# A state space scan: drive by diagonal matmuls on TensorE for half of the groups, and the sum over states by identity matmuls

## Chip, cores, metric

One core of a Trainium2 chip (trn2). The metric is the device time of one execution in microseconds (us), the median of several.

## The reference, cut to what matters

Two layers on an input of 4 x 384 x 64 x 64, all in f32. The first is a state space (Mamba) layer over L = 4096 positions, with 768 inner channels and 16 states each; the second is a neighbourhood attention. Only the first is touched. Its core, after projections and a short convolution that give dt, B, C and xc:

```python
def step(h, inp):
    dt_t, B_t, C_t, x_t = inp
    dA  = jnp.exp(dt_t[:, :, None] * A[None])              # "decay"
    dBx = (dt_t * x_t)[:, :, None] * B_t[:, None, :]       # "drive"
    h   = dA * h + dBx                                     # the scan over positions
    y_t = jnp.einsum('bdn,bn->bd', h, C_t)                 # product with C, sum over the 16 states
    return (h, y_t)
```

## The kernel before

The layer is worked off in 64 *steps* (4 batches x 16 chunks of T = 256 positions). In each, channels lie on the 128 partitions in ND = 6 tiles d, and the 16 states in four groups g of NG = 4. A pair m = (d, g) is one group; each group is scanned in two halves of two states, so that a step has 48 *slots*, one per half. All other work of the layer (projections, convolution, normalization of the coming chunks) is written into a plan that says in which slot it is issued; engines keep that order.

For each group: ScalarE makes the decay, one exponential per state, into PSUM; VectorE or GpSimd makes the drive (dt x) * B; VectorE scans; GpSimd multiplies by C; TensorE sums over the states.

```python
def driven(I, m, h, eng):                      # 15 of 24 on VectorE, 9 on GpSimd
    d, g = divmod(m, NS // NG)
    db = w2.tile([P, NG, T], F32, tag="db", name=f"db_{I}_{m}", bufs=6)
    dtx = dtx_ps[:, d % 2, :] if eng is nc.vector else h["dtx"][d]
    eng.tensor_tensor(db, dtx.unsqueeze(1).broadcast_to([P, NG, T]), h["B"][g], ALU.mult)
    dbs[I, m] = db

def decay(I, m, half, h):
    d, g = divmod(m, NS // NG)
    da = ps_a.tile([P, 2, T], F32, tag="da", name="da")          # PSUM
    for k in range(2):
        n = g * NG + 2 * half + k
        act(da[:, k, :], h["dt"][d // 2][:, d % 2, :], AF.Exp, scale=nega[:, d, n : n + 1])
    das[I, m, half] = da

def scans(I, m, half, hs): ...                 # tensor_tensor_scan(hs, da, db, state, mult, add)
def with_c(I, m, h, hs): ...                   # GpSimd: last state kept; hs = hs * C

def summed(I, m, h, hs):                       # transposes that accumulate in PSUM
    ...
    for k in range(NG):
        for half in range(2):
            nc.tensor.matmul(
                y[:, d % 2, half, :], hs[:, k, half * P : (half + 1) * P], ident,
                is_transpose=True, start=..., stop=..., skip_group_check=True,
            )
# turn(): ScalarE copies the turned sum to SBUF, TensorE turns it back and adds D * xc
```

Transposes by an identity that accumulate in one PSUM bank add the states up, turned; one more transpose for each pair of tiles turns the result back.

## Time and profile before

| | us |
|---|---|
| time, median of all its runs beside the changed kernel's | 8368.6 (8366.0 to 8371.4) |
| layer 0, one step of 64 | 92.4 |
| start and layer 1 | some 2450 |

The busy line and three groups of the page show who does what. PE is TensorE, PEld its weight loads, DVE VectorE, ACT ScalarE and POOL GpSimd; the granted clock, met below, is the share of its full clock that TensorE was given. A group's line gives the operation, output and inputs, shapes, count, busy time and the mean length of one, then the idle time before it.

```profile
PE 7252.0 (87%) x45882; PEld 5495.0 (66%) x45882; DVE 7311.7 (87%) x13300; ACT 5812.2 (70%) x13758; POOL 7092.7 (85%) x5719
```

```profile
L571 DVE TENSOR_TENSOR_SCAN hs<-da,state,db 128x256 f32<-128x256 f32 x5760 | 3855.0, 728 | 88.9 <-ACT da L96 64.8
...
L594 PE MATMUL y<-ident,hs 128*128 128x128 f32 x12288 | 1774.6, 296 | 904.5 <-POOL hs L581 902.3
...
L550 DVE TENSOR_TENSOR db<-dtx_ps,B 128x1024 f32<-128x1024 f32 x960 | 1141.3, 1199 | 0.0
```

The two averages of 87% come from different layers. The scans take the most VectorE time, the drive (L550) comes second there, and that is what the change takes away. The sum (L594) mostly waits for GpSimd.

### The profile page before, as it was taken

To read this page: it belongs to the slowest core of one execution; us is meant where nothing else is said; L and a number is where in the kernel's file an instruction comes from. 1 tells how busy PE (TensorE), PEld (TensorE's weight loads), DVE (VectorE), ACT (ScalarE), POOL (GpSimd) and SP (SyncE) were. 2 spreads that over 40 slices of the span, in tenths; PEclk is the share of its full clock that TensorE was granted. 3 is DMA by queue.
4 is the path that set the end of the run, shared out by engine and by line. 5 is a ranking of instruction groups with operands and counts; after the bars stand their busy time and mean duration, and the time that the engine had idled before them with its cause. 6 is when DMAs were issued, how large, how long until landed. Compare 5 with 4: busy or idle time off the path is not lost. (4 is left out here: it accounts for less than half of the span.)

```text
span 8357.8 us, 139186 instructions
## 1 busy us (share of the span) xinstructions
PE 7252.0 (87%) x45882; PEld 5495.0 (66%) x45882; DVE 7311.7 (87%) x13300; ACT 5812.2 (70%) x13758; POOL 7092.7 (85%) x5719
## 2 busy tenths in 40 slices
PE   7888888888888888888888888888699999999999
PEld 5776677777666677776777677766555555555555
DVE  5999999999999999999999999999856666666666
ACT  5777777777777777777777777777545455455455
POOL 4999999999999999999999999999767677777677
PEclk9998898889889998899898889989799999999999
DMA  3111211121112111211211111112122232232222
GB/s 112 59 61 66 75 58 55 63 74 58 62 66 74 53 58 66 72 58 64 68 63 53 58 65 60 55 57 71 65 89 86 76 94 88 78 92 85 83 87 65
DMA packets 327504, 583.06 MB, mean 70 GB/s; under 512 B 62940, under 2 KB 211180, under 8 KB 326660
## 3 DMA queue, kind: packets, MB, share of 16 engines
q1 hardware_dynamic: 326788, 574.17, 21.3%
q8 instruction: 370, 6.06, 0.3%
q14 instruction: 346, 2.83, 0.1%
HBM read 471.49 MB, written 84.73 MB: 67 GB/s over the span
## 5 line engine op out<-in xcount | busy, mean ns | idle before, releaser
L571 DVE TENSOR_TENSOR_SCAN hs<-da,state,db 128x256 f32<-128x256 f32 x5760 | 3855.0, 728 | 88.9 <-ACT da L96 64.8
L96 ACT ACTIVATE da<-dt,nega 128x256 f32<-128x256 f32 x6144 | 2917.7, 477 | 1208.2 <-DVE hs L571 1100.8
L581 POOL TENSOR_TENSOR hs<-hs,C 128x1024 f32<-128x1024 f32 x1536 | 3621.7, 2358 | 123.9 <-POOL state L580 0.4
L594 PE MATMUL y<-ident,hs 128*128 128x128 f32 x12288 | 1774.6, 296 | 904.5 <-POOL hs L581 902.3
L594 PEld LDWEIGHTS y<-ident,hs 128*128 128x128 f32 x12288 | 1540.5, 153 | 1207.9 <-POOL hs L581 1098.9
L941 POOL TENSOR_SCALAR sg<-sg,rsum 128x308 f32<-128x308 f32 x1536 | 1619.9, 1073 | 633.8 <-DVE rsum L939 631.8
L550 POOL TENSOR_TENSOR db<-dtx,B 128x1024 f32<-128x1024 f32 x576 | 1360.5, 2362 | 0.1
L550 DVE TENSOR_TENSOR db<-dtx_ps,B 128x1024 f32<-128x1024 f32 x960 | 1141.3, 1199 | 0.0
L382 PE MATMUL mm_ps<-xn,w_in 128*128 128x256 f32 x4608 | 1127.4, 392 | 10.1 <-DVE yg L624 8.1
L96 ACT ACTIVATE sg<-sg,mx 128x308 f32<-128x308 f32 x1536 | 828.7, 541 | 251.3 <-DVE mx L926 236.7
L926 DVE CUSTOM_DVE_ANT_0 sg<-lg_ps,bias 128x308 f32<-128x308 f32 x1536 | 643.1, 475 | 375.1 <-PE lg_ps L920 375.1
L382 PEld LDWEIGHTS mm_ps<-xn,w_in 128*128 128x128 f32 x4608 | 872.5, 197 | 119.1 <-DVE yg L624 8.4
L389 PE MATMUL mm_ps<-xb,dcv 128*128 128x256 f32 x3072 | 783.9, 409 | 0.0
L389 PEld LDWEIGHTS mm_ps<-xb,dcv 128*128 128x128 f32 x3072 | 615.7, 208 | 88.3 <-issue 0.3
L969 ACT COPY tb<-pt_ps 88x512 f32<-88x512 f32 x384 | 222.2, 579 | 624.7 <-PE pt_ps L965 624.7
L580 POOL COPY state<-hs 128x4 f32<-128x4 f32 x1536 | 289.1, 188 | 341.8 <-DVE hs L571 328.0
L639 PE MATMUL mm_ps<-yg,w_out 128*128 128x256 f32 x2304 | 539.8, 385 | 0.0
L956 DVE COPY ta<-pt_ps 110x512 f32<-110x512 f32 x768 | 492.4, 682 | 23.2 <-PE pt_ps L951 23.2
L639 PEld LDWEIGHTS mm_ps<-yg,w_out 128*128 128x128 f32 x2304 | 439.6, 195 | 59.1
L951 PE MATMUL pt_ps<-ident,sg 128*110 128x128 f32 x3072 | 417.7, 279 | 0.8 <-POOL sg L941 0.8
L951 PEld LDWEIGHTS pt_ps<-ident,sg 128*110 128x110 f32 x3072 | 322.7, 133 | 77.9 <-issue 47.6
L824 PE MATMUL mm_ps<-xn,w_qkv 128*128 128x512 f32 (+2 forms) x612 | 270.7, 579 | 60.4 <-DVE xn L811 53.2
(141 smaller groups left out, 9152.5 us busy)
## 6 DMA issues: line engine op xcount, KB each, us to landing
B<-bcrows SPq DMA_DIRECT2D x256, 512.0 KB
C<-bcrows SPq DMA_DIRECT2D x256, 512.0 KB
vw<-vd SPq DMA_DIRECT2D x1792, 33.0 KB
xr<-x SPq DMA_DIRECT2D x28, 1056.0 KB
vd<-v SPq DMA_DIRECT2D x280, 96.0 KB
xi<-in_x_dram SPq DMA_DIRECT2D x64, 384.0 KB
xo<-in_x_dram SPq DMA_DIRECT2D x64, 384.0 KB
x<-xo SPq DMA_DIRECT2D x64, 384.0 KB
```

The costliest lines, as they stand in the source:

```text
L96: ins = nc.scalar.activation(o, i, func, **kw)
L382: nc.tensor.matmul(pb[:, k, :], w_in[:, j, m * P : (m + 1) * P], xn[:, j, :], start=(j == 0), stop=(j == NJ - 1),)
L389: nc.tensor.matmul(pb[:, k, :], dcv[:, d, c, :], xb[:, d, c : c + T], start=(c == 0), stop=(c == KC - 1),)
L550: eng.tensor_tensor(db, dtx.unsqueeze(1).broadcast_to([P, NG, T]), h["B"][g], ALU.mult)
L571: nc.vector.tensor_tensor_scan(hs[:, j, :], da[:, k, :], dbs[I, m][:, j, :], state[:, d, n : n + 1] if I % NCHUNK else 0.0, ALU.mult, ALU.add,
L581: nc.gpsimd.tensor_tensor(hs, hs, h["C"][g], ALU.mult)
L594: nc.tensor.matmul(y[:, d % 2, half, :], hs[:, k, half * P : (half + 1) * P], ident, is_transpose=True, start=(first and half == 0 and d % ...
L639: nc.tensor.matmul(h["po", first][:, m - first, :], w_out[:, d, m * P : (m + 1) * P], h["yg"][d // 2][:, d % 2, :], start=(d == 0), stop=( ...
L926: nc.vector.tensor_tensor_reduce(sg[:, hh, :], lg[:, :NK], bias[:, 4 * m + hh, :], -1.0, BIG, ALU.add, ALU.min, mx[:, hh : hh + 1],)
L941: nc.gpsimd.tensor_scalar(sg[:, hh, :], sg[:, hh, :], rs[:, hh : hh + 1], None, ALU.mult)
L951: nc.tensor.transpose(pt[: KN[c], col : col + P], sg[:, 2 * pair + hh, KOFF[c] : KOFF[c] + KN[c]], ident,)
L956: nc.vector.tensor_copy(t[: KN[0], :, :].rearrange("p a q -> p (a q)"), pt[: KN[0], :])
```

## The change

Its intent: VectorE is full in layer 0, so let TensorE make the drive of groups 0 and 2. (dt x) * B over positions t is a matmul of the turned dt x with a diagonal matrix of B, which leaves the drive in PSUM; the decay of these groups then goes to SBUF. The sum over states becomes a matmul by the identity, which needs no turning back.

```diff
-            ps_a = es.enter_context(tc.tile_pool(name="ps_a", bufs=2, space=PSUM))
-            ps_x = es.enter_context(tc.tile_pool(name="ps_x", bufs=1, space=PSUM))
+            ps_a = es.enter_context(tc.tile_pool(name="ps_a", bufs=3, space=PSUM))
...
+            ON_PE = (0, 2)
...                                   # the plan: input projections some seven slots later
-                    ((-10, -9, -6), (1, 2, 5), (9, 10, 13)),
+                    ((-3, -2, 1), (4, 5, 8), (11, 12, 15)),
...                                   # diagonal(g), twice a step, VectorE
+                    nc.vector.tensor_tensor(
+                        h["dg", g],
+                        ident.unsqueeze(1).unsqueeze(1).broadcast_to([P, 2, NG, P]),
+                        h["BT", g][:, :, r0 : r0 + NG].unsqueeze(3).broadcast_to([P, 2, NG, P]),
+                        ALU.mult,
+                    )
...                                   # decay()
+                ps_half = ps_a.tile([P, 2, T], F32, tag="da", name="da")
+                da = ps_half
+                if g in ON_PE:
+                    da = w2.tile([P, 2, T], F32, tag="das", ..., bufs=3)     # SBUF
+                    for th in range(2):
+                        nc.tensor.matmul(
+                            ps_half[:, :, th * P : (th + 1) * P],
+                            h["dtxT", d // 2][:, th, k * P : (k + 1) * P],
+                            h["dg", g][:, th, 2 * half : 2 * half + 2, :],
+                            start=True, stop=True,
+                        )
+                    dbs[I, m, half] = ps_half
...                                   # summed(), now for one half
-                        nc.tensor.matmul(y[...], hs[...], ident, is_transpose=True, ...)
+                for j in (2 * half, 2 * half + 1):
+                    nc.tensor.matmul(
+                        y, ident, hs[:, j, :], start=False,
+                        stop=(g == NS // NG - 1 and j == NG - 1),
+                    )
...                                   # decays and drives issued two halves ahead, sums six slots late
+            AHEAD = 2
+            LAG, FIRST, GATE, HS = 6, 9, 7, 6
```

Left out here: dt x in double width and its transposes, fewer loads of B, the new slots of the 12 drives that stay (4 on VectorE, 8 on GpSimd).

## The prediction

> **What bounds the kernel now.** I read the page's busy line and slices first, then the stretches, then the groups and the waits of one undisturbed stretch (3000 to 4000 us), and last the order of time on TensorE.
>
> ```profile
> PE   7888888888888888888888888888699999999999
> DVE  5999999999999999999999999999856666666666
> PEclk9998898889889998899898889989799999999999
> ```
>
> The two layers are plain in the 40 slices: up to about slice 29 (6030 us) the state space layer, in which VectorE stands at 9, and after it the attention layer, in which TensorE does. The diff touches the first layer alone.
>
> ```profile
> 3000.00:4000.00 1000.00, 844.54 (x4419) 699.60 (x4418) 982.09 (x1433) 786.39 (x1719) 921.44 (x692) 0.89 0.19 64
> 7000.00:8000.00 1000.00, 958.42 (x8539) 568.79 (x8537) 647.41 (x2090) 502.13 (x1560) 719.17 (x704) 1.00 0.29 86
> ```
>
> The columns are TensorE, its weight loads, VectorE, ScalarE and GpSimd, then TensorE's granted clock. In layer 0 VectorE is busy 98%, GpSimd 92%, TensorE 84% at a granted clock of 0.89, ScalarE 79%. The layer makes 64 steps (4 batches x 16 chunks of 256 positions), each with 96 scans. Between 1000 and 6000 us the trace has 5195 decays, so 54.1 steps of 96, which is **92.4 us a step**. 64 x 92.4 = 5914 us; the other 8371 - 5914 = 2457 us (start, layer 1) should not change.
>
> ```profile
> ACT da L96 <- DVE hs L571: 184.6, 266, 2.1
> PEld y L594 <- POOL hs L581: 183.1, 93, 4.0
> PE y L594 <- POOL hs L581: 150.3, 80, 3.8
> DVE hs L571 <- ACT da L96: 12.5, 15, 1.2
> ```
>
> The waits of that millisecond say the same: VectorE waits 12.5 us in all, ScalarE waits for its scans, and TensorE for the product with C on GpSimd. So VectorE sets the pace and TensorE follows. What matters most is how much room TensorE really has, because the change pays VectorE's relief in matmuls. Its busy share hides that: it includes matmuls at half clock and modelled ends. So I took the distances between starts in dense parts:
>
> ```profile
> 3005.73 2.75 PE L382 MATMUL mm_ps<-xn,w_in 128*128 128x256 f32 x12
> 3008.33 1.04 PE L594 MATMUL y<-ident,hs 128*128 128x128 f32 x8
> 3009.20 1.46 PE L382 MATMUL mm_ps<-xn,w_in 128*128 128x256 f32 x6
> ...
> 3029.42 1.46 PE L352 MATMUL mm_ps<-xn,ones_c 128*128 128x256 f32 x6
> 3030.72 1.04 PE L594 MATMUL y<-ident,hs 128*128 128x128 f32 x8
> ```
>
> First column start, second length. Twelve records of the input projection take 3008.33 - 3005.73 = 2.60 us, 216.5 ns each. The program has 36 such matmuls a step and 4608 records in 64 steps, 72: **an f32 matmul is two records, so one with 256 columns costs 433 ns**. Eight transposing matmuls take 3009.20 - 3008.33 = 0.87 us, about 110 ns each, and they are one record each (12288 = 64 x 192). Per column that is 0.86 ns in transposing mode and 1.69 ns as an ordinary matmul. The line of ones_c, where one stationary matrix serves three matmuls in a row, gives 1.30 us for 6 records, 217 ns: reusing the stationary operand saves nothing.
>
> **What the Trainium skill says.** "FP8 and Floating Point Precision", TensorE Precision Notes: true FP32 takes four passes through the array. "TensorE: Matmul & The Clock Gate", Back-to-back issue gap: N/2.4 + 2.5 ns warm, so 109 ns for a pass of 256 columns, and four of them 437 ns (an estimate from that page); the trace's 433 ns agrees. The same page, Part 4 (PE-mode transpose), says transposing does not count as busy for the clock gate; the granted clock of 0.89 in layer 0, full of transposes, against 1.00 in layer 1 at 96% busy is compatible, though layer 1 transposes too and the waits for GpSimd explain it as well. "SBUF", Who interferes with whom: a VectorE instruction with at most one SBUF input does not contend with GpSimd. Both kernels keep one input of each scan in PSUM (the decay before; drive or decay after), so I expect no gain or loss there; no run yet shows it.
>
> **The change, part by part, per step.** Counts are from the instruction orders of both programs, divided by 64.
>
> VectorE. Scans stay at 96; six back to back take 3.86 us, so 0.645 us each, 61.9 us.
>
> ```profile
> 3030.20 3.47 DVE L550 TENSOR_TENSOR db<-dtx_ps,B 128x1024 f32<-128x1024 f32 x3
> 3033.60 0.94 DVE L358 TENSOR_TENSOR xn<-xn,mm_ps 128x768 f32<-128x768 f32 x1
> ```
>
> Three drive products take 3.40 us, 1.133 each. There were 15; 4 stay: -12.5 us. Two diagonal builds of the same 128x1024 size are new: +2.3. VectorE falls from 0.982 x 92.4 = 90.7 to **80.5 us**.
>
> GpSimd. Products with C stay at 24 (2.32 us start to start, plus 0.27 for the state copy: 62.2). Drives go from 9 to 8 (2.32 each: 20.9 to 18.6). Six dt x products of 0.69 become three of double width, about 1.24 each by their slope (estimate). 87.4 falls to **about 84.5 us**.
>
> ScalarE. Six copies to PSUM (0.37) become two, three copies of the turned sum (0.58) become three of the turned dt x: -1.5. The 48 exponentials written to SBUF instead of PSUM should cost about what they do now (128x512 ones: 614 ns SBUF to SBUF, 602 to PSUM). 72.7 becomes **about 71.5 us**.
>
> TensorE, at full clock:
> - Unchanged: 36 input, 24 convolution, 18 output, 6 x, 6 dt, 6 D and 6 mean matmuls, 102 x 0.433 = 44.2.
> - Removed: 192 transposes x 0.11 = 21.1, and 12 turning back, 1.3. So before it needed 66.6 us, 72% of the step.
> - Added: the sum over states as 96 identity matmuls of 256 columns, 96 x 0.433 = 41.6; the drive of half of the groups, 24 halves x 2 x 0.433 = 20.8; 12 transposes of dt x, 1.3; four small ones of B, 0.2.
> - After: 44.2 + 41.6 + 20.8 + 1.5 = **108.1 us**.
>
> So the sum over states costs about twice what the transposing sum did, the drive comes on top, and TensorE needs 108 us a step where the whole step now takes 92.4. VectorE's 10 us become idle time. TensorE's floor for the kernel is 64 x 108.1 + 2457 = 9375 us.
>
> What lies beside other work: I laid each instruction in its slot of the plan (48 slots a step). In the 26 slots from 45 to 22, with all projections and convolutions, TensorE has 70.6 us against 42 to 45 of the others. In the other 22 slots TensorE has 37.5, VectorE 38.7, GpSimd 39.0 and ScalarE about 37.9: nearly even, so TensorE will wait there a little. It cannot run far ahead: the drive of a half needs a PSUM buffer that the scan three halves earlier frees, and the sum needs the product with C. Against that, the others enter this stretch ahead by what buffers allow. The burst of Silu with two table loads (some 6 us of ScalarE without a decay) costs VectorE and then TensorE a few us. The floor by stretches is 70.6 + 39.0 = 109.6; I choose **111 us** for jitter. 64 x 111 + 2457 = 9561, rounded to 9560 us, 14% slower.
>
> **The rivals.**
> (a) VectorE's relief carries: if TensorE were paced as the author hoped, the step would fall to GpSimd's 84.5 plus slack, say 87, and the kernel to 8025. For it: VectorE is busy 98%, and TensorE waits visibly for GpSimd. Against: it needs TensorE to do 108 us of work in 87, an f32 matmul of 348 ns. No dense part of this trace shows that.
> (b) TensorE is the bound and the coupling is tight, so that each few slots take the longest engine's time, not the average. Summing maxima over groups of four slots gives some 120 us a step, 10140 us. For it: three PSUM buffers and sums that lag by only 6 slots. Against: now, with nearly equal loads on VectorE and GpSimd, VectorE still loses only 2%.
> (c) It evens out: the clock. If the half-clock stretches vanish, TensorE gains; but I already count full clock, so this can only miss the other way: should waits keep the clock at 0.89 in the light stretch, that adds up to 37.5 x 0.12 = 4.5 us a step, 9850 us.
>
> **Range and chances.** Low end 9390 is TensorE without a gap; I see no way much below it while f32 matmuls cost 433 ns. High end 9920 is (c), with some of (b). Faster by over 2% needs rival (a): 3%. Within 2% (up to 8540) would need a step of 95 us: 3%. Slower: 94%.
>
> **What would show it.** In layer 0, TensorE over 95% busy at a granted clock near 1.0, VectorE about 73%, GpSimd 76%, ScalarE 65%. The waits turn round: VectorE's scans wait for TensorE's drive, GpSimd for VectorE, while TensorE's waits for GpSimd nearly vanish. The identity matmuls appear as 12288 records of 128x256, at 216 ns start to start, the drive as 6144. Layer 1 keeps its 2330 us. I am wrong on the main step if those records come closer together than 216 ns (then TensorE has room); wrong on the coupling if TensorE is idle over 5% of layer 0; wrong on the ports if the scan grows past 0.645 us with its decay in SBUF.

## The result, and the profile after

Ratios are the mean time of one kernel's runs over that of the other's of the same rounds, so not quite the ratio of the medians quoted.

| | before | after |
|---|---|---|
| median, us | 8368.6 | 9643.8 |
| ratio | | 1.152 (1.150 to 1.154) |
| layer 0, one step | 92.4 | 113.0 |
| layer 1, us | 2331 | 2334 |

The step after is counted as before: 5098 decays between 1000 and 7000 us are 53.1 steps. Layer 1 is counted from the last record of the sum (6026.4 and 7305.5 us) to the end of the span. The slices of the changed kernel, then three of its groups:

```profile
PE   8999999999999999999999999999998999999999
...
DVE  5777777777777777777777767777775666666666
...
PEclk9999999999999999999999999999999999999999
```

```profile
L625 DVE TENSOR_TENSOR_SCAN hs<-da,state,da 128x256 f32<-128x256 f32 x2880 | 1990.2, 733 | 1557.4 <-PE da L605 1195.4
L650 PE MATMUL y<-hs,ident 128*128 128x256 f32 x12288 | 3022.7, 380 | 1.1 <-POOL hs L635 1.1
...
L605 PE MATMUL da<-dg,dtxT 128*128 128x256 f32 x6144 | 1593.1, 383 | 137.3 <-DVE hs L625 134.4
```

The nines have moved from VectorE's row to TensorE's. The sum has as many records as before but each has 256 columns, and its waiting for GpSimd is gone (1.1 us against 902.3); VectorE waits 1195 us before scans whose drive TensorE makes. The stretch of 3000 to 4000 us:

```profile
3000.00:4000.00 1000.00, 981.50 (x4527) 825.49 (x4527) 725.30 (x1095) 615.32 (x1377) 732.44 (x531) 1.00 0.13 42
```

TensorE 98%, at a granted clock of 1.00; VectorE 73%, GpSimd 73%, ScalarE 62%. And the waits there, longest in total first (total, number, longest single one):

```profile
POOL state L634 <- DVE hs L625: 249.5, 113, 4.9
DVE hs L625 <- PE da L605: 181.5, 113, 3.9
ACT da L96 <- DVE hs L625: 138.6, 105, 3.9
```

The chain has turned: GpSimd and ScalarE wait for the scans, the scans for the drive. In a dense part of TensorE's order of time:

```profile
3110.41 1.89 PE L650 MATMUL y<-hs,ident 128*128 128x256 f32 x8
3112.14 1.03 PE L605 MATMUL da<-dg,dtxT 128*128 128x256 f32 x4
3113.00 2.75 PE L650 MATMUL y<-hs,ident 128*128 128x256 f32 x12
```

Eight records of the sum take 1.73 us, four of the drive 0.86: 216 ns each, as the prediction took from other matmuls.

### The profile page after: what moved, and what is told of

Its sections match the earlier page's. It is cut to its first block, busy times and chain, and to the rows that moved or that the text cites.

```text
span 9639.9 us, 151697 instructions
## 1 busy us (share of the span) xinstructions
PE 9335.2 (97%) x52282; PEld 7311.4 (76%) x52282; DVE 6767.6 (70%) x12724; ACT 5604.7 (58%) x13502; POOL 6948.3 (72%) x5463
## 4 chain that ended last, share of the span: by engine, by line
PE 86%; DVE 8%; ACT 3%; issue 1%; POOL 1%; DMA 0%; SPq 0%; DVEq 0%; POOLq 0%; ACTq 0%
PE y L650 23%; PE da L605 12%; PE mm_ps L381 10%; PE mm_ps L388 7%; PE mm_ps L668 5%; PE pt_ps L998 3%; DVE hs L625 3%; PE lg_ps L967 3%; PE mm_ps L871 3%; PE mm_ps L1051 3%; PE mm_ps L904 3%; PE mm_ps L934 3%; PE pv_ps L1024 2%; PE mm_ps L515 2%; PE mm_ps L458 2%; PE pt_ps L1012 2%
## 5 line engine op out<-in xcount | busy, mean ns | idle before, releaser
L635 POOL TENSOR_TENSOR hs<-hs,C 128x1024 f32<-128x1024 f32 x1536 | 3622.1, 2358 | 124.7 <-POOL state L634 1.2
L96 ACT ACTIVATE da<-dt,nega 128x256 f32<-128x256 f32 x6144 | 2777.7, 487 | 1121.8 <-DVE hs L625 1011.2
L625 DVE TENSOR_TENSOR_SCAN hs<-da,state,da 128x256 f32<-128x256 f32 x2880 | 1990.2, 733 | 1557.4 <-PE da L605 1195.4
L650 PE MATMUL y<-hs,ident 128*128 128x256 f32 x12288 | 3022.7, 380 | 1.1 <-POOL hs L635 1.1
L650 PEld LDWEIGHTS y<-hs,ident 128*128 128x128 f32 x12288 | 2320.9, 190 | 356.2 <-issue 45.6
L625 DVE TENSOR_TENSOR_SCAN hs<-da,state,db 128x256 f32<-128x256 f32 x2880 | 1938.9, 727 | 20.2 <-ACT da L96 20.2
L605 PE MATMUL da<-dg,dtxT 128*128 128x256 f32 x6144 | 1593.1, 383 | 137.3 <-DVE hs L625 134.4
L605 PEld LDWEIGHTS da<-dg,dtxT 128*128 128x128 f32 x6144 | 1146.3, 190 | 359.6 <-issue 100.8
L590 POOL TENSOR_TENSOR db<-dtx,B 128x1024 f32<-128x1024 f32 x512 | 1208.3, 2360 | 5.0
L388 PE MATMUL mm_ps<-xb,dcv 128*128 128x256 f32 x3072 | 725.5, 378 | 0.0
L576 ACT COPY dtxT<-mm_ps 128x512 f32<-128x512 f32 x192 | 112.0, 583 | 646.6 <-PE mm_ps L568 646.6
```

The costliest lines, as they stand in the source:

```text
L96: ins = nc.scalar.activation(o, i, func, **kw)
L388: nc.tensor.matmul(pb[:, k, :], dcv[:, d, c, :], xb[:, d, c : c + T], start=(c == 0), stop=(c == KC - 1),)
L605: nc.tensor.matmul(ps_half[:, :, th * P : (th + 1) * P], h["dtxT", d // 2][:, th, k * P : (k + 1) * P], h["dg", g][:, th, 2 * half : 2 * h ...
L625: nc.vector.tensor_tensor_scan(hs[:, j, :], da[:, k, :], db, state[:, d, n : n + 1] if I % NCHUNK else 0.0, ALU.mult, ALU.add,)
L635: nc.gpsimd.tensor_tensor(hs, hs, h["C"][g], ALU.mult)
L650: nc.tensor.matmul(y, ident, hs[:, j, :], start=False, stop=(g == NS // NG - 1 and j == NG - 1),)
```

## The experiments

Twelve runs, each three rounds beside the kernel before on the same chip; every result was correct. For comparison with the working, a measured step is (median - 2412) / 64, where 2412 = 9643.8 - 64 x 113.0; against a count of decays in the traces this is good to about 0.6 us. For the kernel before, the 92.4 is the count itself; the formula would give 93.1, so set the other rows' steps against that where half a microsecond matters. "Need" is TensorE's time at full clock and dense spacing, worked out as in the prediction.

| run | need | step measured | median us | ratio to before |
|---|---|---|---|---|
| before | 66.6 | 92.4 | 8368.6 | 1 |
| identity sum alone (e2) | 85.8 | 93.6 | 8400.9 | 1.004 |
| drive with transposing sum (e1) | 88.9 | 101.8 | 8926.9 | 1.067 |
| changed kernel: both | 108.1 | 113.0 | 9643.8 | 1.152 |
| both, and zero matmuls (e4) | 118.5 | 121.6 | 10191.8 | 1.218 |
| both, sum in bf16 (e5) | 77.0 | 95.8 | 8545.4 | 1.022 |

### First set: take TensorE's costs apart

Theory 1: TensorE's total sets the step. Rivals: the round trip between drive and scan, or the sum alone.

**Drive kept, sum as before (e1).** The changed kernel with the old `summed` and `turn`, in halves:

```diff
-                    nc.tensor.matmul(y, ident, hs[:, j, :], start=False, ...)
+                        nc.tensor.matmul(
+                            y[:, d % 2, th, :], hs[:, k, th * P : (th + 1) * P], ident,
+                            is_transpose=True, ...)
+                    turn(I, p, h, slot_of(I), (p + 1) * (SLOTS // 3) + GATE)
```

> The changed kernel with the transposing sum of the kernel before (drive on TensorE kept). Theory 1, TensorE's throughput: its need falls from 108.1 to 108.1 - 41.6 + 21.1 + 1.3 = 88.9 us a step; with the 4.5% on top that the changed kernel showed (113.0 for 108.1) 92.9 us, so 64 x 92.9 + 2412 = 8360 us, 8250 to 8500, about the time before. Rival, the round trip between the drive and the scan through three PSUM buffers: the waits stay, over 9000. Rival, the identity sum alone is the cause and the drive costs nothing: the step falls to GpSimd's 84.5 plus slack, below 8100.

Measured: 8926.9 us (8922.5 to 8937.5), 1.067 (1.066 to 1.069). This misses every expectation: 717 us better than the changed kernel, but a step of 101.8 us where TensorE needs 88.9 and the kernel before takes 92.4. This kernel's stretch from 3000 to 4000 us, and two of the waits there:

```profile
3000.00:4000.00 1000.00, 933.36 (x5180) 786.20 (x5179) 809.15 (x1228) 700.36 (x1567) 819.09 (x595) 0.98 0.15 47
```

```profile
DVE hs L625 <- PE da L605: 144.0, 97, 3.6
...
PE da L605 <- DVE hs L625: 28.5, 26, 3.4
```

No engine is full. VectorE still waits for drives, and TensorE for scans.

**Identity sum alone (e2).** The kernel before with

```diff
-                        nc.tensor.matmul(y[...], hs[...], ident, is_transpose=True, ...)
+                    nc.tensor.matmul(y, ident, hs[:, j, :], start=False, ...)
-                    turn(I, p, h, slot_of(I), (p + 1) * (SLOTS // 3) + 4)
+                    slot_of(I)((p + 1) * (SLOTS // 3) + 5, lambda ...: gated(I, p, h))
```

> The kernel before with the identity sum alone (no drive on TensorE). Theory 1: TensorE's need rises from 66.6 to 66.6 - 22.4 + 41.6 = 85.8 us a step, still under the 92.4 that VectorE sets: same within 2%, 8370 to 8540. Rival, the identity sum alone is the cause: about 20 us a step more, 9500 or over.

Measured: 8400.9 us (8394.4 to 8402.1), 1.004 (1.003 to 1.006), as theory 1 says. Some 19 us of TensorE work more in each step cost 0.4%, because VectorE still sets the pace:

```profile
3000.00:4000.00 1000.00, 956.98 (x4278) 807.46 (x4277) 977.47 (x1424) 769.48 (x1672) 913.36 (x687) 0.98 0.19 61
```

TensorE is at 96% and VectorE at 98%: the clock of 0.89 before has become 0.98, so TensorE's earlier 84% had room that did not show.

**More TensorE work (e4).** The changed kernel with one more matmul per group:

```diff
...                                   # zeros: a matrix of zeros; one buffer fewer for gated tiles, to fit
+                if half == 0:
+                    nc.tensor.matmul(y, zeros, hs[:, 0, :], start=False, stop=False)
```

> The changed kernel with one matmul more for each group, by a matrix of zeros into the same sum (right result). Theory 1: 24 x 0.433 = 10.4 us a step more, all on the path: 9644 + 665 = 10310 us, 10250 to 10370. Rival, waits between engines set the step: the matmuls fall into TensorE's waits, under 9850.

Measured: 10191.8 us (10191.0 to 10194.2), 1.218 (1.217 to 1.220), just below the range of theory 1. Of 10.4 us added per step 8.6 arrive in the time (548 us of 665). The rival (under 9850) falls: in the changed kernel TensorE's time is on the path, nearly one to one.

**Less TensorE work (e5).** Products with C written as bf16, summed with a bf16 identity; coarser on purpose:

```diff
-                nc.gpsimd.tensor_tensor(hs, hs, h["C"][g], ALU.mult)
+                nc.gpsimd.tensor_tensor(hb, hs, h["C"][g], ALU.mult)          # hb is bf16
-                        y, ident, hs[:, j, :], start=False,
+                        y, ident_b, hbs[I, m][:, j, :], start=False,
```

> The changed kernel with the products with C written as bf16 and summed with a bf16 identity (coarser on purpose). If a bf16 matmul of 256 columns is one pass of 109 ns, TensorE's need falls to 108.1 - 41.6 + 10.5 = 77.0 us a step, under GpSimd's 84.5, which then sets the step with 3 to 6% on top: 87 to 90 us, 7980 to 8170. Rival, round trip of the drive: over 9000. The result's error may be too large.

Measured: 8545.4 us (8540.4 to 8552.4), 1.022 (1.020 to 1.024). The pass count is right: four records of the sum are 0.43 us apart start to start, 108 ns each, one for each state. But the step is 95.8, not 87 to 90, and the rival's 9000 us is missed too. (To fit, `hs` has 3 buffers here instead of 6 and the bf16 tile 5; what that costs was not tested.) Two rows of TensorE's order of time:

```profile
3069.33 0.60 PE L655 MATMUL y<-hb,ident_b 128*128 128x256 bf16 x4
3069.76 1.46 PE L384 MATMUL mm_ps<-xn,w_in 128*128 128x256 f32 x6
```

Together with e1: as soon as TensorE has room, something else costs some 10 us a step, and only kernels with the drive on TensorE show it (e2 does not). These kernels also share the changed plan of slots, and e2 has the old one; no run has the drive without the new plan or the new plan without the drive, so the two are not told apart.

### Second set: does the output projection crowd one long stretch?

The prediction had split a step into 26 slots full of projections and 22 light ones. The sums of the longest engine in each (109.6, 118.5, 98.5 and 92.8 us for the changed kernel, e4, e1 and e5) each lie some 3 us under the measured steps, which looked like an explanation (theory 2). It says what moving work must do.

**Output projection moved, transposing sum (e6)**, the edit below on e1 (with one buffer more for the gated tiles and one less for decays, to fit SBUF):

```diff
-                for n, slot in enumerate((17, 18, 19, 20, 21, 22)):
+                for n, slot in enumerate((27, 28, 29, 30, 32, 33)):
```

> The changed kernel with the transposing sum, and the output projection moved from slots 17 to 22 into slots 27 to 33. Theory 2, the longest engine of each stretch: TensorE's 60.2 us in the 26 slots 45 to 22 lose 18 x 0.433 = 7.8 and stay the longest there with 52.4; its 28.7 in the other 22 slots become 36.5, still under GpSimd's 39.0; plus the 3.2 us that the four runs so far showed: 94.6 us a step, 64 x 94.6 + 2412 = 8470 us, 8380 to 8600. Theory 1, TensorE's total of the step alone: nothing removed, so as the transposing sum without the move, 8927.

Measured: 8943.1 us (8927.7 to 8943.7), 1.069 (1.067 to 1.070): no gain at all. **The same on the changed kernel (e7)**

> The changed kernel with the output projection moved alone (identity sum). Theory 2: 70.6 - 7.8 = 62.8 and 37.5 + 7.8 = 45.3, now both set by TensorE, 108.1 + 3.1 = 111.2 us a step, 9530 us, 1% less than the 9644 of the changed kernel. Theory 1 says 9644, so this run hardly tells them apart; it shows whether 108.1 us is a floor: not under 9450.

took 9705.5 us (9703.2 to 9707.6), 1.160 (1.158 to 1.162), 0.6% more than without. **The same on the bf16 sum (e9)**

> The bf16 sum with the output projection moved (coarser on purpose). Theory 2: TensorE's 53.8 becomes 46.0 against GpSimd's 45.4, its 23.3 becomes 31.1 under 39.0: 46.0 + 39.0 + 3.2 = 88.2 us a step, 8060 us. Theory 1: as without the move, 8545.

took 8551.1 us (8549.3 to 8561.4), 1.022 (1.021 to 1.024), no gain. Theory 2 is dead: four numbers had fitted, and three runs that it should have sped up did not move.

**One group of four on TensorE (e8)**, as a kernel that might beat both: `ON_PE = (0,)`, transposing sum, 18 drives left (9 on each of VectorE and GpSimd), the output projection moved.

> An attempt at a kernel faster than both: drive on TensorE for one group of four, transposing sum, output projection moved. TensorE 78.5 us a step (46.8 and 31.7 by stretch), VectorE 85, GpSimd 87 (about 47 and 40 by stretch). Theory 2: 47 + 40 + 3.2 = 90.2 us a step, 8185 us, 2% under the kernel before. If the drive costs by its round trip and not by TensorE's time, over 8500.

Measured: 8760.3 us (8754.0 to 8762.7), 1.047 (1.045 to 1.049). TensorE needs only 78.5 us here, in a step of 99.2; theory 2's 8185 fails, and the time lies where the rival put it (over 8500).

### Third set: short crowded stretches

Theory 3: the drive ties the engines together more closely than that, so that short crowds count. I laid the instructions into their slots, with durations from the traces, and for every window of eight neighbouring slots took the engine with most work in it; the mean of this over all 48 windows, times 48/8, is a step. The width of eight was chosen because it fits the runs so far, so the fit proves nothing yet:

| | changed | e1 | e4 | e5 | e6 | e7 | e8 | e9 | e2 | before |
|---|---|---|---|---|---|---|---|---|---|---|
| windows of 8 | 111.8 | 101.6 | 120.0 | 95.5 | 101.3 | 112.8 | 99.2 | 95.4 | 97.1 | 94.7 |
| measured | 113.0 | 101.8 | 121.6 | 95.8 | 102.0 | 114.0 | 99.2 | 95.9 | 93.6 | 92.4 |

The two kernels without a drive on TensorE do better than the windows, as windows of 12 to 16 slots. Redone from the instruction order of these kernels and median spacings in their traces, windows of eight give 112.2, 98.4, 121.1, 92.6, 100.2, 113.8, 97.7, 93.9, 96.6 and 93.4: the same picture, but up to 3.2 us lower for kernels with the drive, and there a width of six fits better (100.3 for e1, 93.9 for e5). So the width is known only roughly. The test is a plan that does the same work in other slots.

**Even plan (e10)**: e6 with the projections, convolutions and drives in slots for which the windows give 95.3 us.

```diff
-                    ((-3, -2, 1), (4, 5, 8), (11, 12, 15)),
-                    ((0, 1, 4), (6, 7, 10), (14, 15, 18)),
-                    ((3, 4, 7), (9, 10, 13), (15, 16, 19)),
+                    ((-4, -3, 0), (1, 2, 5), (11, 12, 15)),
+                    ((-3, -2, 1), (4, 5, 8), (14, 15, 18)),
+                    ((9, 10, 13), (19, 20, 23), (16, 17, 20)),
...                          # likewise softplus (33, 36, 50), output projection (25 to 28, 35, 36), drives
```

> Transposing sum and drive on TensorE as in the first experiment, the same instructions, but projections, convolutions and drives spread over other slots so that no stretch of eight slots is crowded (and no more than three PSUM banks of the shared pool are in use at a time). Theory 3, the drive ties TensorE, VectorE, ScalarE and GpSimd together within about eight slots, and each such stretch takes its longest engine's time: the sum of the maxima over eight slots, 101.6 us a step for the first experiment (measured 101.8), is 95.3 here: 64 x 95.5 + 2412 = 8525 us, 8440 to 8620. Theory 2 (two long stretches): as the output projection's move, no change, 8930. Theory 1 (TensorE's total): 8930.

Measured: 8480.1 us (8472.2 to 8482.9), 1.014 (1.012 to 1.015): a step of 94.8 for 95.3 worked out. The same engines do the same work 447 us sooner than in e1. The new plan also keeps to three banks of the shared PSUM pool. From 1000 to 6000 us of e6, TensorE waits for the gate on VectorE (L677) to free such a bank before it turns dt x (L568):

```profile
PE mm_ps L568 <- DVE yg L677: 79.2, 43, 1.8
```

That is 1.6 us a step, and e10 has no such wait. So spreading the work and freeing banks changed together; what each gave is not shown.

**Even plan for one group (e12)**, the same on e8, windows 91.7 us.

> The attempt with one group on TensorE, its plan spread in the same way. Sum of maxima over eight slots 91.7 us a step (before the spreading 99.2, measured 99.2): 64 x 91.7 + 2412 = 8280 us, 8200 to 8400, about 1% under the kernel before. Theory 2 and theory 1: 8760 as before the spreading.

Measured: 8301.3 us (8297.2 to 8302.0), 0.992 (0.991 to 0.994): a step of 92.0 for 91.7. It is the only exact kernel here that beats the kernel before, by 0.8%, which is clear of the noise.

**Further ahead (e11), less far ahead (e13)**: what ties the engines? On e10,

```diff
-            AHEAD = 2
+            AHEAD = 3            # e11; also ps_a with 4 banks, the shared pool with 3
+            AHEAD = 1            # e13; nothing else
```

> The even plan with one PSUM bank moved from the shared pool to the drives (4 instead of 3) and drives issued three halves ahead instead of two. If the width of the stretch is set by how far ahead the drive may be, it widens: the sum of maxima over twelve slots is 93.7 us, 8410, at least 60 us under the even plan. If not, the same as the even plan within 30 us.

> The even plan with decays and drives issued one half ahead instead of two, PSUM banks as they were. The run with three ahead was mixed up with a smaller shared pool (TensorE's projections waited for banks). If the lead sets how tightly the engines are tied: slower than the even plan's 8480, by the sums of maxima over six or four slots 98 to 103 us a step, 8700 to 9030. If the lead does not matter: 8480 within 40 us.

Measured: e11 8758.5 us (8752.5 to 8759.2), 1.047 (1.045 to 1.048), much slower; e13 8362.7 us (8361.7 to 8363.3), 1.000 (0.998 to 1.001), *faster* than the even plan by 117 us. Both go against what I expected: in these two runs, issuing drives earlier does not loosen anything. e11 is mixed up with its smaller pool (TensorE there waits 18 us in the millisecond for VectorE before an input projection, which e10's list of TensorE's waits does not have), so it settles nothing alone. Nor does it give a drive more room: with four buffers and three ahead, a drive still needs the buffer of the scan just before the current half, as in e10 (four buffers and two ahead was not run). e13 changes one number. Stretch from 3000 to 4000 us, and the drive's waits between 1000 and 6000 us, first of e10:

```profile
3000.00:4000.00 1000.00, 978.14 (x5520) 830.97 (x5519) 860.64 (x1311) 750.55 (x1673) 877.40 (x636) 0.99 0.17 53
```

```profile
DVE hs L625 <- PE da L605: 226.2, 171, 3.0
...
PE da L605 <- DVE hs L625: 99.6, 79, 2.4
```

Then the same two views of e13:

```profile
3000.00:4000.00 1000.00, 989.29 (x5634) 839.08 (x5633) 880.96 (x1336) 761.40 (x1704) 890.46 (x647) 1.00 0.17 54
```

```profile
DVE hs L625 <- PE da L605: 303.4, 253, 3.4
...
PE da L605 <- DVE hs L625: 52.5, 61, 4.4
```

The scans wait *longer* for drives (303 us against 226), yet the kernel is faster. TensorE waits half as long for scans (52.5 against 99.6) and is at 98.9%. Per step that wait is 0.9 us shorter, half of the 1.8 us gained; drive records also follow each other faster, 219 ns from start to start (idle time taken off) against 225, another 0.6. The rest is open. A drive needs a PSUM buffer. With three buffers and two ahead it is the one of the scan just before the current half, with one ahead that of the scan before it, finished longer ago. The Trainium skill, "TensorE: Matmul & The Clock Gate", Step-by-step, says that matmuls stay in program order and only weight loads are pulled ahead; if so, all matmuls behind a waiting drive wait too. The halved wait agrees with this; the queue itself is not seen in the trace.

e13 also bears on e1. With another plan and a lead of one, the work of e1 (need 88.9) fills TensorE and takes a step of 93.0: the 92.9 that theory 1 had expected of e1. So the work alone did not make e1 slow.

## Why the prediction was right

The direction, the bound and the range were right; the time was 9643.8 for 9560. Three slips in its working moved nothing: the 12.5 us is VectorE's wait for decays alone (its idle time in that millisecond is 1000 - 982.09 = 17.9), ScalarE's 72.7 - 1.5 is 71.2, and the low end of 9390 is 15 us above the floor of 9375. The half clock that it speaks of is in the trace: the clock of the kernel before steps between full and half, and a record of the input projection takes 379 ns at the median and 796 at most.

- **The bound moves to TensorE: shown.** It is 98% busy in layer 0 at clock 1.00 (predicted over 95% near 1.0). e4 shows its time on the path, e1 and e5 that taking its work away shortens the kernel.
- **433 ns for an f32 matmul of 256 columns, 110 for a transpose of 128: shown.** Eight records of the sum take 1.73 us; e5 gives 108 ns when one pass is enough. 12288 and 6144 records were there as counted.
- **The sum over states costs double and the drive comes on top: right as TensorE time.** As kernel time the two do not add: the sum alone +0.4% (hidden beside VectorE), drive with its plan alone +6.7%, both +15.2%. That need for both to go over 92.4 us was the prediction's arithmetic (85.8, 88.9, 108.1). But by that arithmetic the drive alone would have been nearly free, and that is wrong by 560 us.
- **108.1 us of need, 1.5 for the stretches, 1.4 for jitter: 113.0 measured.** From one start to the next, idle time taken off (1000 to 7000 us), records of the sum took 221 ns and of the drive 220 instead of 216.5 (0.9 and 0.4 us a step), those of the dt and x projections 264 and 239 (0.8), the input projection's 219 (0.2), and TensorE was idle 1.9% (2.1): 4.4 of the 4.9 us. The rest is in small matmuls that the need rounds off or leaves out. That the 2.9 us on top came near is partly luck: 1.5 came from the stretches, which fall below, and 1.4 was a guess.
- **VectorE's relief becomes idle time: right.** Predicted 80.5 us of 111 busy; 0.725 x 113 = 82 measured. GpSimd 84.5 predicted, 0.732 x 113 = 83 measured; ScalarE 71.5 and 70.
- **No gain or loss at the ports: right.** Scans with drive in PSUM and decay in SBUF have the same median, 724 ns, as the others and as before (no run has a scan with both in SBUF, so the rule about the ports is not tested). Minimum, median and maximum in ns:

```profile
L625 DVE TENSOR_TENSOR_SCAN hs<-da,state,da x2880: 715/724/749, 216.8 to 7294.0; 128x256 f32<-128x256 f32 x192
L625 DVE TENSOR_TENSOR_SCAN hs<-da,state,db x2880: 712/724/751, 220.8 to 7296.6; 128x256 f32<-128x256 f32 x192
```

- **Rival (a) fell:** f32 matmuls are no faster. **Rival (c) did not come about:** the clock was 1.00. **Rival (b), tight coupling,** was too strong with groups of four slots (120); eight fit (111.8). In the changed kernel it hides behind TensorE's total. Where TensorE has room, it is the best account here of what the drive together with its plan costs: e10 and e12 came out as windows of eight said, e11 and e13 did not.
- **The split into 26 and 22 slots** gave a good number for a wrong reason, which is luck. Work moved from the crowded to the light stretch (e7) made the kernel slower.

Open: what sets the width of eight slots. The number ahead is not it in the way I thought; the order of TensorE's queue may have a part (e13), its size is not separated from that of the other engines, which keep the order of the plan too. Whether the drive or the slots that came with it cost e1 its time, and how much of e10's gain is PSUM banks, is open as well. An even plan with one ahead for one group on TensorE may be better than 8301 us; it was not run.

## What to carry to other kernels

Before moving work to an engine with "room", count its need from the spacing of starts in dense parts, not from its busy share, and compare the sum after the change with the whole step. An engine put inside the loop of the bottleneck (here: drive, scan, buffer, drive) should also have its work spread evenly, and buffers free in time; the same work in other slots made 447 us of difference here. Issuing such work earlier need not help: the buffer that it needs may not be free by then, and here a lead of one beat a lead of two by 117 us.

## What the Trainium skill lacked or had wrong

- "TensorE: Matmul & The Clock Gate", Terms, calls the transposing mode 4 times faster for FP32. Here it is twice: 110 ns for 128 columns against 433 ns for 256 in an ordinary f32 matmul, 0.86 and 1.69 ns per column. The stationary matrix does not set the 110: in layer 1 of the kernel before, transposes with 110 and 88 of its columns instead of 128 (L951, L965) are as far apart, 109 ns at the median. Summing the 16 states by accumulating transposes therefore costs half of what identity matmuls cost: a need of 21.1 + 1.3 us a step against 41.6.
- The same page, Part 4 (PE-mode transpose), says that transposing does not count as busy for the clock gate. Mixed with matmuls, transposes did not keep the clock low: e13 makes more transposes a step than the kernel before (the same 192 and 12, and 12 of dt x) and has a granted clock of 1.00 in the stretch shown, against 0.89 before. It also idles less there (1.1% against 15.5%) and makes more ordinary matmuls, so which of these keeps the clock up, and whether transposing lowered it before, is not shown.
- "FP8 and Floating Point Precision", TensorE Precision Notes, has the four passes of FP32; I found no page that says that a trace shows them as two records of 216 ns each, while a transpose or a bf16 matmul is one.
- "ScalarE: Activation LUTs", Step-by-step, says that writing PSUM is faster than SBUF, with no figure at that place (other pages give access overheads by memory). In the changed kernel the mean exponential of 128x256 took 476 ns into PSUM and 499 into SBUF, told apart by their order in the trace; all together 477 before and 487 after.
- I found no page that gives GpSimd's cost for a narrower output: the product with C of 128x1024 took 2358 ns to f32 and 2359 to bf16.
